# The second copy of the short lists' places: in three PSUM banks, or in the product's SBUF buffer

## The chip, the cores and the metric

One core of one Trainium2 chip runs the kernel once. The metric is the device time in microseconds (us); the runs of a kernel are compared by their median. The profile shows one execution: "span" is the time from the first to the last instruction of the program, less than the device time of a run.

Engines are named as in the profile: PE is TensorE, PEld its weight loads, DVE VectorE, ACT ScalarE, POOL GpSimd, SP SyncE. SBUF and PSUM are the two on-chip memories. PSUM is used here in banks of 512 float32 per partition, eight in all.

## The reference, cut to what matters

Two layers over 16 graphs of 1024 nodes with 64 channels. Layer 0 multiplies the adjacency (rows divided by their sums) with the normalised nodes. Layer 1 takes, for each node and channel, three quantiles over the node's neighbours, after some neighbours are dropped, and puts the weighted sum through a small network.

```python
# layer 0
h = jnp.maximum(_layernorm(x, axis=-1), 0.0)
x = x + jnp.matmul(A / clip(sum(A, 2), 1.0), h)
# layer 1
h = jnp.maximum(_layernorm(x, axis=-1), 0.0)
adj_d = _dilate_adj(adj, mask)            # drops every skip-th neighbour of long lists
vals = jnp.where((adj_d > 0)[..., None], h[:, None, :, :], big)
sv = jnp.sort(vals, axis=2)
for tau, wt in zip([0.25, 0.5, 0.75], [0.25, 0.5, 0.25]):
    q = gather(lo) * (1.0 - frac) + gather(hi) * frac   # lo, hi: places around tau * (m - 1)
    agg = agg + wt * q
x = x + relu((h + agg) @ W1 + b1) @ W2 + b2
```

`x` is (16, 1024, 64), `adj` (16, 1024, 1024), all float32; most nodes have few neighbours, a few have many.

## The kernel before, in words

The list path does the work; a dense path behind a flag runs only if a list overflows.

**Layer 0**, batch by batch: adjacency rows are loaded (`at`), ACT takes their signs (`sg`), DVE turns the signs into keyed neighbour lists (`rec`), PE transposes the rows into `pt` banks, ACT copies these to `att`, PE multiplies them with the nodes into a `ps_small` bank, and so on to a record per node (`row`). POOL scatters the records to DRAM (`srt`), sorted by list length, one indirect DMA for each 128 rows.

**Layer 1**, in four groups of four batches. A group's nodes are cut into ten classes by list length (the lists of `CAPS`); each class is a `Job` with T tiles of 128 nodes and n places each, the node itself included. There are 40 such short jobs. Four more jobs (`LONG`) take the longest lists of all batches. A job does this:

- POOL gathers each place's channels by an indirect DMA into `places` (`lplaces` for the long lists), one DMA for each place and tile, 124 in each group.
- DVE finds the dropped places (`rem`, `gone`, `ok`), ACT adds a huge number to them.
- DVE sorts along the places with a network of `tensor_tensor` min and max passes. A pass reads two runs of places and writes a third; so that a pass never overwrites what another still needs, each place exists in two copies: copy 0 is `places`, copy 1 is `other` (`long_other` for the long lists), copy 2 the node itself (`S`).
- DVE and ACT multiply the sorted places with the weights `w`, which gives `prod`. PE sums and transposes `prod` through an identity into a `pt` bank, and the small network follows in `ps_small` banks; POOL scatters the result (`out_dram`).

For the short lists `other` is one PSUM tile of three banks (`ps_o`), one buffer. For the long lists `long_other` lies in SBUF, and after about 0.8 us of passes (`BREATH`) a one-element memset of `idle` stands between them. `prod` (SBUF, two buffers) is taken after the passes, before the product. `pt` has two banks, `ps_small` three.

**The order** is made by a planner (`Plan`). Every stream of work yields an engine and the earliest time at which it could go on; the planner keeps a modelled clock for each engine and always issues the stream that could begin first. `room(name, bufs)` is that time for a buffer: infinite while its last users haven't released it. On DVE and POOL this order is kept as written; the instructions of ACT, PE and SP are ordered by the compiler's scheduler, by their data dependencies. All of these engines execute in order. All operations go through a recording helper, so that the profile has line 228 for nearly all of them, and groups are told apart by tile names.

The steps of the prediction can be followed at these places: the pools at the start of `list_path`; `transposes`, `products` and `layers`, which take `pt` and `ps_small`; `Job.sort`, which takes `other` and `prod`, makes the passes and the product; `Job.run`, which issues the gathers.

Of the kernel before, what the change touches and what calls it, by code (L numbers as in the profile page):

```python
# [9 lines left out]
F32 = mybir.dt.float32  # L10
# [8 lines left out]
P = 128  # L19
# [18 lines left out]
)  # L38
CAPS2 = [CAPS[1]] + CAPS[2::2]
LONG = (88, 31, 24, 20)  # L40
LSEG = 8
LCAPS = (24, 16, 16, 16)
LSUB = 8
# [168 lines left out]
INF = float("inf")  # L212
BREATH = 0.8
# [20 lines left out]
class Plan:  # L234
# [33 lines left out]
    def at(self, *tiles):  # L268
        return max(self.ready.get(t.tensor.name, INF) for t in tiles)
# [104 lines left out]
def list_path(ctx, tc, x, adj, nodemask, w1, b1, w2, b2, out, go):  # L374
# [23 lines left out]
    gat = ctx.enter_context(tc.tile_pool(name="gat", bufs=3))  # L398
    tiny = ctx.enter_context(tc.tile_pool(name="tiny", bufs=2))
    mlp = ctx.enter_context(tc.tile_pool(name="mlp", bufs=2))  # L400
    ps_t = ctx.enter_context(tc.tile_pool(name="ps_t", bufs=2, space=bass.MemoryType.PSUM))
    ps_s = ctx.enter_context(tc.tile_pool(name="ps_s", bufs=3, space=bass.MemoryType.PSUM))
    ps_o = ctx.enter_context(tc.tile_pool(name="ps_o", bufs=1, space=bass.MemoryType.PSUM))


    diff = consts.tile([P, P], I32, name="diff")
# [149 lines left out]
    def known(st, *names):  # L556

        return max(at(st[name]) if name in st else INF for name in names)
# [19 lines left out]
    def beginnings(pool, now):  # L578

        for b, st in enumerate(batch):  # L580
            now[0] = b
            yield "DVE", lambda: max(known(st, "xt", "mrow"), room("h0", 3), room("row", 4))
            mrow_f = new(tiny, [NT, P], F32, "mrow_f", 2)
            nc.vector.tensor_copy(mrow_f, st["mrow"])

            h0 = new(pool, [P, NT, C + 1], F32, "h0", 3, users=2)
            nc.vector.memset(h0[:, :, C:], 1.0)
            row = st["row"] = new(pool, [P, NT, RW], F32, "row", 4, users=1)
            nc.vector.memset(row[:, :, C:W], -1.0)
            yield from normed(h0[:, :, :C], st["xt"])  # L590
            st["h0"] = h0
            yield "PE", lambda: max(at(mrow_f), room("ps_small", 3))
            pm = new(ps_s, [P, HALF], F32, "ps_small", 3, users=1)
            nc.tensor.transpose(pm[:, :NT], mrow_f, ident[:NT, :NT])
            yield "ACT", lambda: at(pm)
            nc.scalar.copy(row[:, :, RW - 1], pm[:, :NT])
            nc.scalar.copy(row[:, :, RW - 2], row_f)
            free(pm)
# [58 lines left out]
    def transposes(pool, now):  # L657
        for b, st in enumerate(batch):
            now[0] = b
            for t in range(NT):  # L660
                hf, k = divmod(t, BPH)
                for h2 in range(2):
                    yield "PE", lambda: max(
                        at(st["rows"][t]) if t in st["rows"] else INF, room("pt", 2),
                        0.0 if hf in st["att"] else room("att", 2),
                    )
                    if hf not in st["att"]:
                        st["att"][hf] = new(pool, [P, NT, HALF], F32, "att", 2, users=1)
                    pt = new(ps_t, [P, HALF], F32, "pt", 2, users=1)
                    for q in range(BPH):  # L670
                        c0 = (h2 * BPH + q) * P
                        nc.tensor.transpose(
                            pt[:, q * P:(q + 1) * P], st["rows"][t][:, c0:c0 + P], ident
                        )
                    plan.add(turned(st, hf, k, h2, pt), 10 * b + 3)
                free(st["rows"][t])

    def products(pool, now):


        for b, st in enumerate(batch):
            now[0] = b
            for hf in range(2):
                yield "PE", lambda: INF if st["copied"][hf] < 2 * BPH else max(
                    at(st["att"][hf]), known(st, "h0"), room("ps_small", 3)
                )
                po = new(ps_s, [P, HALF], F32, "ps_small", 3, users=1)
                for q in range(NT):
                    if q and q % 2 == 0:
                        yield "PE", always  # L690
                    nc.tensor.matmul(
                        po[:C + 1, :], st["h0"][:, q, :], st["att"][hf][:, q, :],
                        start=(q == 0), stop=(q == NT - 1),
                    )
                free(st["att"][hf])
                free(st["h0"])
                yield "ACT", lambda: max(at(po), room("msg", 2))
                msg = new(pool, [C + 1, HALF], F32, "msg", 2)
                nc.scalar.copy(msg, po[:C + 1, :])
                free(po)  # L700
                yield "PE", lambda: max(at(msg), room("ps_small", 3))
                pb = new(ps_s, [P, HALF], F32, "ps_small", 3, users=1)
                sums = pb[:, :BPH * (C + 1)].rearrange("p (k c) -> p k c", c=C + 1)
                for k in range(BPH):
                    nc.tensor.transpose(
                        sums[:, k, :], msg[:, k * P:(k + 1) * P], ident[:C + 1, :C + 1]
                    )
                yield "DVE", lambda: at(pb) + SLACK
                x1 = st["row"][:, hf * BPH:(hf + 1) * BPH, X1:R0]
                deg = new(tiny, [P, BPH], F32, "deg", 2)  # L710
                nc.vector.tensor_scalar(deg, sums[:, :, C], 1.0, None, op0=OP.max)
                nc.vector.reciprocal(deg, deg)
                nc.vector.tensor_tensor(
                    x1, sums[:, :, :C], deg.unsqueeze(2).to_broadcast([P, BPH, C]), OP.mult
                )
                nc.vector.tensor_tensor(
                    x1, x1, st["xt"][:, hf * BPH:(hf + 1) * BPH, :], OP.add
                )
                free(pb)
                st["residual"] += 1  # L720
            free(st["xt"])
# [15 lines left out]
    def endings(pool, now):  # L737

        first = lambda rank: rank - 3000
        for b, st in enumerate(batch):  # L740
# [28 lines left out]
            nc.vector.tensor_tensor(  # L769
                hot, cls, d.unsqueeze(1).to_broadcast([P, CLS, NT]), OP.is_equal  # L770
            )
            yield "PE", lambda: max(at(hot), room("ps_small", 3))
            pc = new(ps_s, [P, HALF], F32, "ps_small", 3, users=1)
            K = CLS * NT
            flat = hot.rearrange("p c t -> p (c t)")
            nc.tensor.matmul(pc[:, :K], earlier, flat, start=True, stop=True)
# [54 lines left out]
    class Job:  # L831
# [50 lines left out]
        def sort(self):  # L882
# [41 lines left out]
            else:  # L924
# [10 lines left out]
            nc.scalar.activation(u, u, AF.Abs)  # L935
            nc.scalar.activation(u, u, AF.Relu, bias=wt0, scale=-QUANTILES[0][1])
            yield "DVE", lambda: max(
                at(A) + SLACK if helped else 0.0, room("prod", 2) if short else 0.0,
                room("other" if short else "long_other", 1),
            ), self.later  # L940
            if short:
                Bt = new(ps_o, [P, 3 * HALF], F32, "other", 1, users=1)
                other = Bt[:, :n * T * C].rearrange("p (k t c) -> p k t c", k=n, t=T)
            else:
                other = Bt = new(pool, [P, n, T, C], F32, "long_other", 1, users=1)

            def places(copy, run, shift=0):
# [16 lines left out]
            for op, ai, aj, dist, copy, run in ops:  # L964
# [9 lines left out]
                nc.vector.tensor_tensor(dst, a, c, op)  # L974
                plan.own = None
                done.update(((copy, i + shift), plan.clock["DVE"] + 0.15) for i in each)
                if not short:

                    since += 0.07 + len(each) * T * C * 1.04e-3
                    if since > BREATH:  # L980
                        nc.vector.memset(idle, 0.0)
                        since = 0.0
            yield "DVE", lambda: at(u) + SLACK, self.later

            w = new(pool, [P, count, T], F32, name + "w", bufs)
# [1 line left out]
            nc.vector.scalar_tensor_tensor(w, u[:, 2, :, :], 2.0, w, op0=OP.mult, op1=OP.add)  # L987
            free(u)

            total = max(count + 1, 4)  # L990
            prod = None
            if short:
                prod = new(pool, [P, T, total, C], F32, "prod", 2, users=1)
                if count + 1 < total:
                    nc.vector.memset(prod[:, :, count + 1:, :], 0.0)

            helped = plan.clock["ACT"] < plan.clock["DVE"] + 2.0
            for copy in (1, 0):
# [20 lines left out]
                    )  # L1019
            if short:  # L1020
                free(A)
                free(Bt)
                if not helped:
                    yield "ACT", lambda: at(S)
                nc.scalar.copy(prod[:, :, count, :], S[:, :, :C])
# [13 lines left out]
        def layers(self, terms, sources):  # L1039

            T, R = self.T, terms[0][0].shape[1]
            yield "PE", lambda: max(at(*sources) + LOOSE, room("y", 6), room("pt", 2))
            y = new(mlp, [P, T, CO], F32, "y", 6, users=1)
            x1 = y
            if self.short:
# [3 lines left out]
            for t0 in range(0, T, 4):  # L1049
                ts = range(t0, min(t0 + 4, T))  # L1050
                M = len(ts) * P
                if t0:
                    yield "PE", lambda: room("pt", 2)
                pt = new(ps_t, [P, HALF], F32, "pt", 2, users=1)
                for i, t in enumerate(ts):
                    for k, term in enumerate(terms[t]):
                        nc.tensor.matmul(
# [7 lines left out]
                ot = new(mlp, [2 * C, HALF], F32, "ot", 2)  # L1065
                nc.scalar.copy(ot[:R, :M], pt[:R, :M])
                free(pt)
                yield "PE", lambda: max(at(ot) + SLACK, room("ps_small", 3))
                ph = new(ps_s, [P, HALF], F32, "ps_small", 3, users=1)
                nc.tensor.matmul(ph[:, :M], w1_sb[:R, :], ot[:R, :M], start=True, stop=True)  # L1070
                yield "ACT", lambda: max(at(ph) + SLACK, room("hid", 2))
                hid = new(mlp, [H, HALF], F32, "hid", 2)
                nc.scalar.activation(hid[:, :M], ph[:, :M], AF.Relu, bias=b1_sb)
                free(ph)
                yield "PE", lambda: max(at(hid) + SLACK, room("ps_small", 3))
                py = new(ps_s, [P, HALF], F32, "ps_small", 3, users=1)
                pv = py[:, :len(ts) * CO].rearrange("p (t c) -> p t c", c=CO)
                nc.tensor.matmul(
                    py[:, :len(ts) * CO], ones_f[:1, :], b2_sb[:, :len(ts) * CO],
# [554 lines left out]
```

## Time and profile before

| | |
|---|---|
| runs | 1948.59, 1953.29, 1955.87 us; median 1953.29 |
| profiled execution, span | 1511.0 us; its own device time isn't recorded apart; the median lies 442.3 us above the span |
| PE, PEld busy | 738.8, 464.7 us |
| DVE busy | 1191.3 us (79%), 4104 instructions |
| ACT busy | 816.4 us (54%) |
| POOL busy | 957.2 us (63%), 1154 instructions, 931 of them indirect DMAs |
| DMA | 133.36 MB, 88 GB/s in the mean |
| granted PE clock, mean | 0.699 |

How to read it: layer 0 runs from the start to about 890 us, in the later part mixed with the jobs of the first groups; after that there are only jobs. The page's groups give operation, tiles, count, busy time, the mean of one in ns, and the engine's idle time in front of them with what ended it; "issue" is idle time in which the profile shows no wait. The busy tenths cut the span into 40 slices of 37.8 us.

### The profile page before, as it was taken

The page shows a single profiled execution, that of the slowest core. Times are in us where ns is not written, and L with a number is a line of the kernel's source. Part 1 is how long each engine was busy: PE and PEld are TensorE (multiplying, and loading weights), DVE is VectorE, ACT ScalarE, POOL GpSimd, SP SyncE. Part 2 cuts the span into 40 slices and gives each one's busy share as a digit, 9 for nine tenths or more (in the row PEclk, how much of TensorE's full clock was granted, in tenths as well). Part 3 has the DMA queues.
Part 4 walks back from the last instruction along what each step waited for, and adds up shares of the span by engine and source line. Part 5 has one row for each costly group of instructions (what it writes and reads, how often), then busy time and mean ns, then how long its engine had stood idle before and what let it go on. Part 6 is the DMA issues. An engine that isn't in the chain of part 4 may idle for free. (4 is left out here: it accounts for less than half of the span.)

```text
span 1511.0 us, 15983 instructions
## 1 busy us (share of the span) xinstructions
PE 738.8 (49%) x3192; PEld 464.7 (31%) x3192; DVE 1191.3 (79%) x4104; ACT 816.4 (54%) x2789; POOL 957.2 (63%) x1154
## 2 busy tenths in 40 slices
PE   4778777327877556567667620024000123228542
PEld 2434334214544233343444320012000122216432
DVE  6777798997899779859869869893059999986875
ACT  7989878557879457757975520201050223148341
POOL 0122227777678757757777787667777777765083
PEclk8889888658888777869688755555555565558765
DMA  5445665424355253355341242111111111211010
GB/s 177 150 142 168 163 210 160 123 73 114 101 162 152 59 174 94 99 126 161 94 140 31 60 101 68 50 37 28 30 26 23 28 28 40 44 33 22 2 25 13
DMA packets 135718, 133.36 MB, mean 88 GB/s; under 512 B 100756, under 2 KB 103444, under 8 KB 135492
## 3 DMA queue, kind: packets, MB, share of 16 engines
q1 hardware_dynamic: 102876, 90.79, 20.8%
q0 software_dynamic: 32736, 41.47, 11.2%
q14 instruction: 78, 0.64, 0.1%
q8 instruction: 28, 0.46, 0.1%
HBM read 112.90 MB, written 23.61 MB: 90 GB/s over the span
## 5 line engine op out<-in xcount | busy, mean ns | idle before, releaser
L228 POOL DMA_INDIRECT places<-tab,idx x372 | 370.2, 995 | 131.7 <-issue 101.8
L228 PE MATMUL pt<-ident,prod 128*128 128x128 f32 (+1 forms) x736 | 160.2, 377 | 517.8 <-DVE prod L228 241.2
L228 PEld LDWEIGHTS pt<-ident,prod 128*128 128x128 f32 (+1 forms) x736 | 129.3, 256 | 550.4 <-ACT prod L228 412.4
L228 PE MATMUL ps_small<-att,h 128*65 128x512 f32 x512 | 254.7, 644 | 27.3 <-ACT h L228 10.5
L228 POOL DMA_INDIRECT srt<-row,to x128 | 125.9, 984 | 165.8 <-ACT row L228 144.0
L228 PE MATMUL pt<-ident,at 128*128 128x128 f32 x1024 | 176.7, 320 | 96.0 <-ACT att L228 71.1
L228 POOL DMA_INDIRECT lplaces<-whole,lidx x163 | 167.2, 1026 | 55.6 <-issue 48.5
L228 DVE MAX8 rec<-sg 128x8 f16<-128x256 f16 x512 | 180.1, 414 | 4.4
L228 PEld LDWEIGHTS pt<-ident,at 128*128 128x128 f32 x1024 | 136.9, 164 | 143.5 <-ACT att L228 93.8
L228 ACT ACTIVATE sg<-at 128x1024 f16<-128x1024 f32 x128 | 134.8, 1054 | 75.0 <-DMA at<-in_adj_dram 65.7
L228 ACT COPY att<-pt 128x512 f32<-128x512 f32 x256 | 141.9, 582 | 20.7 <-PE pt L228 18.8
L228 POOL DMA_INDIRECT places<-tab,last_idx x124 | 123.8, 998 | 41.3 <-issue 35.0
L228 PEld LDWEIGHTS ps_small<-att,h 128*65 128x65 f32 x512 | 74.7, 151 | 161.9 <-issue 123.2
L228 ACT ACTIVATE places<-places,gone 128x64 f32<-128x64 f32 x496 | 123.5, 335 | 0.5
L228 ACT ACTIVATE prod<-places,w 128x64 f32<-128x64 f32 x213 | 54.1, 336 | 120.5 <-DVE w L228 120.5
L228 POOL DMA_INDIRECT out_dram<-y,nodes_i x93 | 91.8, 987 | 22.6 <-issue 15.1
L228 DVE TENSOR_TENSOR sg<-sg,keyed 128x1024 f16<-128x1024 f16 x128 | 87.2, 681 | 23.7 <-ACT sg L228 23.7
L228 ACT ACTIVATE gone<-gone 128x15 f32<-128x15 f32 (+9 forms) x40 | 8.2, 206 | 169.2 <-DVE ok L228 169.0
L228 DVE TENSOR_TENSOR long_other<-lplaces 128x512 f32<-128x512 f32 (+5 forms) x124 | 64.1, 555 | 29.1 <-ACT lplaces L228 28.9
L228 DVE TENSOR_TENSOR other<-places,other 128x64 f32<-128x64 f32 (+6 forms) x204 | 69.6, 341 | 5.9
L228 PE MATMUL ps_small<-ot,w_sb 128*128 128x128 f32 (+3 forms) x112 | 47.6, 513 | 44.2 <-DVE y L228 31.2
L228 DVE TENSOR_TENSOR places<-places,other 128x64 f32<-128x64 f32 (+2 forms) x208 | 62.3, 309 | 4.9
(231 smaller groups left out, 1670.8 us busy)
## 6 DMA issues: line engine op xcount, KB each, us to landing
at<-in_adj_dram SPq DMA_DIRECT2D x128, 512.0 KB
places<-tab,idx POOLq DMA_INDIRECT x372, 2.5
whole<-tab SPq DMA_DIRECT2D x4, 1057.0 KB
tab<-row SPq DMA_DIRECT2D x16, 264.0 KB
xt<-in_x_dram SPq DMA_DIRECT2D x16, 256.0 KB
lplaces<-whole,lidx POOLq DMA_INDIRECT x163, 2.4
srt<-row,to POOLq DMA_INDIRECT x128, 2.7
places<-tab,last_idx POOLq DMA_INDIRECT x124, 2.4
```

What stands on the lines that cost most here:

```text
L228: ins = getattr(self._engine, op)(*args, **kwargs)
```

## The change

The second copy of the short lists moves from PSUM to SBUF. `other` is now a view of the job's `prod` buffer, which is therefore taken before the passes and held through them; `ps_o` and its three banks go. The buffer is as large as the larger of the two uses. The product of copy 1 is made in place. The one-element memsets now stand between the passes of short lists too. Two of the three banks go to `pt` (2 to 4) and one to `ps_small` (3 to 4), and every `room` of these names follows. The gathers, the passes and their order within a job, the products and the long lists are as before.

```diff
+PT, SMALL = 4, 4
...
-    ps_t = ctx.enter_context(tc.tile_pool(name="ps_t", bufs=2, space=bass.MemoryType.PSUM))
-    ps_s = ctx.enter_context(tc.tile_pool(name="ps_s", bufs=3, space=bass.MemoryType.PSUM))
-    ps_o = ctx.enter_context(tc.tile_pool(name="ps_o", bufs=1, space=bass.MemoryType.PSUM))
+    ps_t = ctx.enter_context(tc.tile_pool(name="ps_t", bufs=PT, space=bass.MemoryType.PSUM))
+    ps_s = ctx.enter_context(tc.tile_pool(name="ps_s", bufs=SMALL, space=bass.MemoryType.PSUM))
...
-                        at(st["rows"][t]) if t in st["rows"] else INF, room("pt", 2),
+                        at(st["rows"][t]) if t in st["rows"] else INF, room("pt", PT),
...
-                    at(st["att"][hf]), known(st, "h0"), room("ps_small", 3)
+                    at(st["att"][hf]), known(st, "h0"), room("ps_small", SMALL)
...
             yield "DVE", lambda: max(
-                at(A) + SLACK if helped else 0.0, room("prod", 2) if short else 0.0,
-                room("other" if short else "long_other", 1),
+                at(A) + SLACK if helped else 0.0, room("prod", 2) if short else room("long_other", 1),
             ), self.later
+            total = max(count + 1, 4)
             if short:
-                Bt = new(ps_o, [P, 3 * HALF], F32, "other", 1, users=1)
-                other = Bt[:, :n * T * C].rearrange("p (k t c) -> p k t c", k=n, t=T)
+                prod = new(pool, [P, T, max(n, total), C], F32, "prod", 2, users=1)
+                other = prod.rearrange("p t k c -> p k t c")
             else:
+                prod = None
                 other = Bt = new(pool, [P, n, T, C], F32, "long_other", 1, users=1)
...
-                if not short:
-
-                    since += 0.07 + len(each) * T * C * 1.04e-3
-                    if since > BREATH:
-                        nc.vector.memset(idle, 0.0)
-                        since = 0.0
+                since += 0.07 + len(each) * T * C * 1.04e-3
+                if since > BREATH:
+                    nc.vector.memset(idle, 0.0)
+                    since = 0.0
...
-            total = max(count + 1, 4)
-            prod = None
-            if short:
-                prod = new(pool, [P, T, total, C], F32, "prod", 2, users=1)
-                if count + 1 < total:
-                    nc.vector.memset(prod[:, :, count + 1:, :], 0.0)
+            if short and count + 1 < total:
+                nc.vector.memset(prod[:, :, count + 1:total, :], 0.0)
...
             if short:
                 free(A)
-                free(Bt)
...
-                yield "PE", lambda: max(at(ot) + SLACK, room("ps_small", 3))
-                ph = new(ps_s, [P, HALF], F32, "ps_small", 3, users=1)
+                yield "PE", lambda: max(at(ot) + SLACK, room("ps_small", SMALL))
+                ph = new(ps_s, [P, HALF], F32, "ps_small", SMALL, users=1)
```

More of the change, by code (lines that the diff above doesn't have):

```diff
@@ L591, in beginnings @@
             st["h0"] = h0
-            yield "PE", lambda: max(at(mrow_f), room("ps_small", 3))
-            pm = new(ps_s, [P, HALF], F32, "ps_small", 3, users=1)
+            yield "PE", lambda: max(at(mrow_f), room("ps_small", SMALL))
+            pm = new(ps_s, [P, HALF], F32, "ps_small", SMALL, users=1)
             nc.tensor.transpose(pm[:, :NT], mrow_f, ident[:NT, :NT])
@@ L668, in transposes @@
                         st["att"][hf] = new(pool, [P, NT, HALF], F32, "att", 2, users=1)
-                    pt = new(ps_t, [P, HALF], F32, "pt", 2, users=1)
+                    pt = new(ps_t, [P, HALF], F32, "pt", PT, users=1)
                     for q in range(BPH):
@@ L684, in products @@
                 yield "PE", lambda: INF if st["copied"][hf] < 2 * BPH else max(
-                    at(st["att"][hf]), known(st, "h0"), room("ps_small", 3)
+                    at(st["att"][hf]), known(st, "h0"), room("ps_small", SMALL)
                 )
-                po = new(ps_s, [P, HALF], F32, "ps_small", 3, users=1)
+                po = new(ps_s, [P, HALF], F32, "ps_small", SMALL, users=1)
                 for q in range(NT):
@@ L700, in products @@
                 free(po)
-                yield "PE", lambda: max(at(msg), room("ps_small", 3))
-                pb = new(ps_s, [P, HALF], F32, "ps_small", 3, users=1)
+                yield "PE", lambda: max(at(msg), room("ps_small", SMALL))
+                pb = new(ps_s, [P, HALF], F32, "ps_small", SMALL, users=1)
                 sums = pb[:, :BPH * (C + 1)].rearrange("p (k c) -> p k c", c=C + 1)
@@ L771, in endings @@
             )
-            yield "PE", lambda: max(at(hot), room("ps_small", 3))
-            pc = new(ps_s, [P, HALF], F32, "ps_small", 3, users=1)
+            yield "PE", lambda: max(at(hot), room("ps_small", SMALL))
+            pc = new(ps_s, [P, HALF], F32, "ps_small", SMALL, users=1)
             K = CLS * NT
@@ L1041, in layers @@
             T, R = self.T, terms[0][0].shape[1]
-            yield "PE", lambda: max(at(*sources) + LOOSE, room("y", 6), room("pt", 2))
+            yield "PE", lambda: max(at(*sources) + LOOSE, room("y", 6), room("pt", PT))
             y = new(mlp, [P, T, CO], F32, "y", 6, users=1)
@@ L1052, in layers @@
                 if t0:
-                    yield "PE", lambda: room("pt", 2)
-                pt = new(ps_t, [P, HALF], F32, "pt", 2, users=1)
+                    yield "PE", lambda: room("pt", PT)
+                pt = new(ps_t, [P, HALF], F32, "pt", PT, users=1)
                 for i, t in enumerate(ts):
@@ L1074, in layers @@
                 free(ph)
-                yield "PE", lambda: max(at(hid) + SLACK, room("ps_small", 3))
-                py = new(ps_s, [P, HALF], F32, "ps_small", 3, users=1)
+                yield "PE", lambda: max(at(hid) + SLACK, room("ps_small", SMALL))
+                py = new(ps_s, [P, HALF], F32, "ps_small", SMALL, users=1)
                 pv = py[:, :len(ts) * CO].rearrange("p (t c) -> p t c", c=CO)
```

## The prediction

> **What bounds the kernel now.** I read the page's busy times and slices first, then POOL's and ACT's waits, then the timeline and group tables of single stretches.
>
> ```profile
> span 1511.0 us, 15983 instructions
> ...
> POOL 0122227777678757757777787667777777765083
> ...
> L228 POOL DMA_INDIRECT places<-tab,idx x372 | 370.2, 995 | 131.7 <-issue 101.8
> L228 POOL DMA_INDIRECT lplaces<-whole,lidx x163 | 167.2, 1026 | 55.6 <-issue 48.5
> ...
> L228 DVE TENSOR_TENSOR other<-places,other 128x64 f32<-128x64 f32 (+6 forms) x204 | 69.6, 341 | 5.9
> ```
>
> DVE has the highest busy share (79%), but look at POOL's slices: from the sixth on they stand at 7 to 8 tenths and don't move, whatever the others do. That is a full queue: a gather takes 0.95 us and 0.30 us of "issue" follow, and 0.95/1.25 is 76%. The timeline shows POOL's real waits (over 2 us): 213 us until the fourth batch is through layer 0, then, up to 1391 us, waits that sum to some 55 us, the longest 12.3, 9.2 and 7.0 us. So nearly all of 1178 us goes to some 850 indirect DMAs in a row. Behind it comes a tail of some 110 us, in which DVE sorts the last long lists.
>
> ```profile
> POOL srt L228 <- ACT row L228: 134.7, 8, 63.7
> ...
> ACT msg L228 <- PE ps_small L228: 4.7, 4, 1.9
> ...
> ACT att L228 <- PE pt L228: 3.4, 12, 0.4
> ```
>
> These are waits of the first 215 us. POOL's start is set by ACT (`row`), which is busy 86 and 89% in the first two hundreds of us; ACT waits for PE little.
>
> **The change part by part.** *Gathers beside the passes.* Today a short pass mostly has one operand in PSUM; after the change both are in SBUF, as in the long sort today. The trace shows what POOL makes of either. The first row is from 1230 to 1250 us, where DVE does nothing but a short sort (17.9 of 19.7 us busy), the second from 1119 to 1171 us, all long sort (51.9 of 52 us):
>
> ```profile
> L228 POOL DMA_INDIRECT places<-tab,last_idx x15 | 14.2, 945 | 4.6 <-issue 4.0 <-DMA places<-tab,last_idx 0.3 <-ACT places L228 0.3
> ```
>
> ```profile
> L228 POOL DMA_INDIRECT lplaces<-whole,lidx x35 | 41.8, 1195 | 10.7 <-issue 10.7
> ```
>
> A gather costs 250 ns more beside passes that read SBUF twice. In the timeline it is seen in each one:
>
> ```profile
> 508.75 0.48 DVE L228 TENSOR_TENSOR places<-places,other 128x128 f32<-128x128 f32 x2
> 508.92 0.94 POOL L228 DMA_INDIRECT places<-tab,idx  x1 [0.30 <-issue]
> ...
> 1142.95 0.68 DVE L228 TENSOR_TENSOR long_other<-lplaces 128x512 f32<-128x512 f32 x1
> 1142.97 0.06 DVE L228 MEMSET idle<- 128x1 f32 x1
> 1143.06 1.38 POOL L228 DMA_INDIRECT lplaces<-whole,lidx  x1 [0.30 <-issue]
> ```
>
> The memsets don't prevent it: they are in that stretch. Price from above: 35 gathers by 0.250 us in 52 us of passes is 0.168 us for each us of them. The passes that read `other` take 69.6 + 62.3 + 55.0 + 50.1 = 237 us (728 of them), the products from it 25.9 us: 263 us by 0.168 is 44 us. Price from below: short jobs already have passes with both inputs in SBUF (the first layers, 208 passes). Going through the timeline gather by gather, the 33 covered to more than 80% by such passes take 1034 ns in the mean, the 155 covered by passes that read PSUM 952 ns: 82 ns. Gathers lie beside PSUM-reading passes for 192.5 us in all, 202 gathers' worth: 17 us. The passes that change are 326 ns long in the mean (237/728), those 208 some 351 ns, the groups of the long ones 448 to 567 ns; so the lower row is the nearer, and I take 20 us. Not all reaches the end: the 55 us of waits behind 213 us can swallow a late POOL where the awaited work isn't late itself. I let a quarter vanish: **+15 us**, bounds +5 and +44.
>
> [...]
>
> *The passes themselves and the memsets.*
>
> ```profile
> L228 DVE TENSOR_TENSOR other<-places,other 128x64 f32<-128x64 f32 x88 | 20.1, 228 | 2.7
> ...
> L228 DVE TENSOR_TENSOR lplaces<-long_other 128x64 f32<-128x64 f32 x13 | 2.8, 218 | 0.0
> ...
> L228 DVE MEMSET idle<- 128x1 f32 x195 | 11.5, 59 | 0.0
> ```
>
> At equal width a pass gains 0 to 10 ns: 728 by 0.005 us is 4 us less DVE work. The rule of `BREATH`, applied to the ten pass lists of a group (234 passes), gives 60 memsets, 240 in all: 240 by 59 ns is 14 us more. Net +10 us on DVE, hidden where POOL is the later one; DVE is 85 to 91% busy from 200 to 600 us and so partly uncovered. I take **+5 us**, bounds 0 and +14.
>
> [...]
>
> *`prod` before the passes.* A sort now begins only when the `prod` of the job but one before has been read by PE. In the timeline, the first pass of a job comes 4.0 to 187 us after that point in all 38 cases, so the wait never binds in today's order: 0; without this cover at most one sort's length (299 us over 40 jobs: 7 us) for a job. Behind such a wait stands all of DVE, the listing of layer 0 among it.
>
> *ACT's copy of the node into `prod`.* It needs no sort today: it ran 0.4 to 167 us ahead of the job's weights in 38 of 40 jobs. In the seven classes with more places than products its slot is now a place being sorted, so ACT waits for passes there: a new wait, with copies to `att`, signs and the next job's masks queued behind it. The scheduler can put it late; ACT already waits for `w` in 13 jobs. I take 0; from above, 28 jobs by the 4.4 us that such a wait costs between 215 and 890 us (17.4 us, 4 times) is 123 us of ACT, which has some 200 us idle there: a quarter on the path is +30 us.
>
> *Two second copies, more banks.* With one `other` the next sort must follow the product before; a dozen jobs follow within 4 us, so there is nearly nothing to gain: -1 us. `pt` banks: over the whole span PE waits 74.4 us for ACT's `att` copies, but ACT only 18.8 us for PE; banks let PE run ahead of an engine that is already the later one. In the first 215 us the two ACT waits shown sum to 8 us, the most that POOL's start can gain. The fourth `ps_small` bank meets 42.7 us of PE waits for `y`, 7 times, 28.6 of them after 890 us, where PE has much idle time. I take **-4 us** for banks and copies, bounds 0 and -63 (8 plus all 55 us of POOL's waits).
>
> Sum: +15 + 5 + 0 + 0 - 4 = +16 us. The span goes from 1511.0 to 1527, and with the same 442.3 us around it the time from 1953.29 to **1969 us**. A difference counts as one from 0.5%, 9.8 us, on; no change is 1943.5 to 1963.1.
>
> **The rivals.** *The banks win (faster).* The fourth small bank frees the products and networks of layer 0 from waiting for `y`, records reach POOL earlier, and POOL's waits close. For it: 55 us of waits are there, several behind ACT and DVE results of layer 0. Against it: ACT and DVE, not banks, are the late ones. It decides when it brings more than 30 us (20 to cover the two costs, 10 to be seen): half of the 55 us and all 8 us at the start are 35, so 1953 + 20 - 35 = 1938 us. Chance 0.21.
>
> *Swallowed (no change).* Narrow passes hold POOL up by the lower price, 17 us, half vanishes in its waits, the memsets hide, the banks bring 4: 1953 + 8 - 4 = 1957 us. Against it: the waits that would swallow it end on DVE and ACT work that gets later too. Chance 0.19.
>
> *ACT stalls (much slower).* The node copy blocks ACT in layer 0 and adds its +30: 1953 + 16 + 30 = 1999 us. For it: the copies run far ahead today. Against it: ACT is only 54% busy. Chance 0.12.
>
> *The forecast*, a fuller POOL queue, 1963 to 1990 us: 0.48. Slower is thus 0.60, the same 0.19, faster 0.21. All orders are made anew by the planner, so that single waits move. The range is 1938 to 2000 us: down to the faster case, up to the ACT case. The forecast's own range is 1963 to 1990.
>
> **What would show it.** Right: gathers beside short sorts at 1030 to 1200 ns instead of 945; POOL's busy time up by 17 to 44 us at the same 931 indirect DMAs; some 435 `idle` memsets; POOL's start at 205 to 213 us; the tail as long as now. Wrong: gathers unchanged beside short passes; or POOL's waits behind 213 us well under 55 us, or a start before 200 us (the banks won); ACT waiting tens of us at the copy from `S` (the ACT case). The planner's new order alone could move a long list's sort into the tail or out of it, which I can't price.

## The result and the profile after

| | median | ratio to the kernel before, 95% interval |
|---|---|---|
| before | 1954.58 us (4 runs) | |
| changed | 2013.02 us (2007.68 to 2019.38, 4 runs) | 1.0307 [1.0280, 1.0334] |

The change costs 3.1%, some 60 us, against a forecast of 16 and a range that ended at 2000. One run of the experiments below, of the changed kernel, took 1660.91 us at a lower granted clock (0.529, the others 0.672 to 0.680) and is left out there. From the page of the changed kernel: span, POOL's tenths, and the two groups that answer to those shown of before (busy time, mean ns, idle time in front).

```profile
span 2005.7 us, 16248 instructions
...
POOL 0232643735371745555716465667577204653051
...
L229 POOL DMA_INDIRECT places<-tab,idx x372 | 364.0, 979 | 253.1 <-issue 106.5
...
L229 DVE TENSOR_TENSOR prod<-places,prod 128x64 f32<-128x64 f32 (+6 forms) x204 | 67.0, 335 | 29.5 <-remote 16.4
```

Nearly everything is wrong with this against the forecast. The gathers' mean fell (995 to 979 ns) where it should have risen, POOL is idle for 253 us in front of them instead of 132, its tenths swing between 1 and 7 where they were to stand still, and the span is 2 us below this execution's own 2007.68 us, not 442. The largest waits of POOL between 215 and 1400 us after the `issue` ones:

```profile
POOL places L229 <- ACT prod L229: 70.1, 4, 37.8
POOL gat_rows L229 <- DVE nodes_i L229: 44.6, 2, 27.0
POOL out_dram L229 <- DVE y L229: 44.4, 5, 27.9
```

POOL waits here for ACT and DVE in turn. The added memsets are as priced, 435 of 59 ns:

```profile
L229 DVE MEMSET idle<- 128x1 f32 x435 | 25.7, 59 | 0.7 <-DVE lplaces L229 0.7
```

### The profile page after: what moved, and what is told of

It is laid out like the page before. It is cut to its first block, busy times and chain, and to the rows that moved or that the text cites. A ratio compares the mean times of both kernels' runs of the same rounds, so it can differ in the third digit from the quotient of the medians.

```text
span 2005.7 us, 16248 instructions
## 1 busy us (share of the span) xinstructions
PE 793.3 (40%) x3192; PEld 508.8 (25%) x3192; DVE 1156.6 (58%) x4343; ACT 831.6 (41%) x2810; POOL 947.7 (47%) x1158
## 4 chain that ended last, share of the span: by engine, by line
DVE 29%; issue 21%; another core or an unknown queue 16%; ACT 13%; PE 11%; POOL 5%; DMA 3%; SPq 1%; DVEq 0%; POOLq 0%; ACTq 0%
PE ps_small L229 6%; PE pt L229 5%; DVE prod L229 5%; DVE places L229 4%; DVE long_other L229 3%; DVE lplaces L229 3%; ACT sg L229 3%; DVE rec L229 2%; POOL places L229 2%; ACT lplaces L229 2%; DMA at<-in_adj_dram 2%; ACT places L229 2%; ACT ln_sq L229 2%; ACT att L229 1%
## 5 line engine op out<-in xcount | busy, mean ns | idle before, releaser
L229 POOL DMA_INDIRECT places<-tab,idx x372 | 364.0, 979 | 253.1 <-issue 106.5
L229 PE MATMUL pt<-ident,prod 128*128 128x128 f32 (+1 forms) x736 | 179.4, 411 | 637.9 <-DVE prod L229 351.6
L229 PEld LDWEIGHTS pt<-ident,prod 128*128 128x128 f32 (+1 forms) x736 | 145.2, 286 | 671.1 <-DVE prod L229 285.4
L229 PE MATMUL ps_small<-att,h 128*65 128x512 f32 x512 | 263.1, 663 | 25.8 <-ACT att L229 17.7
L229 POOL DMA_INDIRECT srt<-row,to x128 | 130.0, 1016 | 204.0 <-ACT row L229 156.0
L229 POOL DMA_INDIRECT lplaces<-whole,lidx x163 | 158.8, 974 | 91.6 <-issue 49.4
L229 PEld LDWEIGHTS pt<-ident,at 128*128 128x128 f32 x1024 | 150.6, 174 | 200.7 <-ACT att L229 99.0
L229 PE MATMUL ps_small<-ot,w_sb 128*128 128x128 f32 (+3 forms) x112 | 56.1, 594 | 159.9 <-ACT ot L229 129.8
L229 ACT ACTIVATE prod<-places,w 128x64 f32<-128x64 f32 x234 | 59.3, 334 | 110.1 <-DVE w L229 94.5
L229 ACT COPY ot<-pt 128x128 f32<-128x128 f32 (+3 forms) x56 | 22.1, 396 | 198.8 <-remote 92.7
L229 DVE TENSOR_TENSOR prod<-places,prod 128x64 f32<-128x64 f32 (+6 forms) x204 | 67.0, 335 | 29.5 <-remote 16.4
```

Source lines behind the costliest of these rows:

```text
L229: ins = getattr(self._engine, op)(*args, **kwargs)
```

## The experiments

Each ratio is to the kernel before on the same chip at the same time. "Told" and "not told" is about the planner: whether its clock counts the memsets, and so whether they change the order that it makes.

### First: the kernel before once more, and one part undone or done alone

The kernel before, unaltered. 

> The kernel before, unchanged, profiled once more. Its first profile has a span of 1511.0 us, 442 us under its runs, and no stall on DVE without a releaser; the profile of the changed kernel has a span of 2005.7 us, 2 us under its run, and 341 us of DVE stalls (over 0.4 us) whose releaser the profile doesn't know. Theory A (stalls of the instruction supply: both kernels have them, and the first profile of before missed them): span 1945 to 1960 us, 250 to 350 us of such stalls on DVE. Theory B (the stalls are new with the change, and the 442 us lie outside the program): span 1505 to 1515 us again, no such stalls. Time ratio to before 1.00 in both.

Measured: 1952.57 us, 0.9988 [0.9964, 1.0012]. From its page (span, the chain's shares by engine, POOL's tenths, the gathers):

```profile
span 1952.3 us, 15983 instructions
...
POOL 0132355462555446356653655576677024574061
...
DVE 33%; ACT 18%; issue 15%; another core or an unknown queue 15%; PE 10%; POOL 5%; DMA 3%; SPq 0%; DVEq 0%; ACTq 0%; POOLq 0%
...
L228 POOL DMA_INDIRECT places<-tab,idx x372 | 359.0, 965 | 224.2 <-issue 107.3
```

The same kernel, with busy times on DVE, ACT and POOL that agree to some 2%, is 441 us longer than in the profile from which the prediction was made. Those 441 us are idle time inside the span, and for much of it the profile names no releaser: "issue" and "another core or an unknown queue" have 30% of the chain. Summed over the trace, gaps of DVE above 0.4 us without a known releaser are 254 us; in the first profile they were 2.5. Part of that can be the trace: it holds 10,504 semaphore updates where the first profile holds 25,405, and a wait whose update is missing has no releaser either. POOL's waits above 2 us behind 215 us sum to 597 us (44 of them) against 113 (13) by the same count. What it looks like, from the timeline, ACT masking a long list's places, here

```profile
1406.02 0.35 ACT L228 ACTIVATE lplaces<-lplaces,lgone 128x64 f32<-128x64 f32 x1 [1.05 <-issue]
...
1407.42 0.59 ACT L228 ACTIVATE lplaces<-lplaces,lgone 128x64 f32<-128x64 f32 x2 [1.05 <-issue]
...
1410.21 0.35 ACT L228 ACTIVATE lplaces<-lplaces,lgone 128x64 f32<-128x64 f32 x1 [1.05 <-issue]
```

and in the first profile:

```profile
1097.78 3.45 ACT L228 ACTIVATE lplaces<-lplaces,lgone 128x64 f32<-128x64 f32 x14
```

Fourteen in 3.45 us there, one or two at a time with a pause of 1.05 us here. A missing record doesn't explain these pauses: POOL had issued the gathers of the masked places 121 to 127 us earlier. So the page shown before and the times shown before are of two different situations. POOL is the bound in the first and not in the second. Theory A has its numbers; that the supply of instructions is what stands isn't shown.

Only the old banks (changed kernel otherwise):

```diff
-PT, SMALL = 4, 4
+PT, SMALL = 2, 3
```

> The changed kernel with pt and ps_small at 2 and 3 banks as before; three banks stay empty. If the new banks (through the planner's new order) cost the 58 us: ratio 1.00 to 1.01. If the move to SBUF, with its memsets and the buffer held through the passes, costs it: ratio 1.025 to 1.035. If the banks helped and hid part of the loss: above 1.035.

Measured: 1961.49 us, 1.0029 [0.9992, 1.0067].

Changed kernel without the short lists' memsets:

```diff
-                since += 0.07 + len(each) * T * C * 1.04e-3
+                if not short:
+                    since += 0.07 + len(each) * T * C * 1.04e-3
...
```

> The changed kernel without the memsets between short passes (239 DVE instructions less). If DVE is short of instructions or time, and the memsets add to it: ratio 1.015 or lower. If POOL is held up by passes that read SBUF twice and the memsets let it in: slower than the changed kernel, 1.035 or more, with gathers beside short passes well over 1044 ns. If neither matters: 1.025 to 1.035.

Measured: 1959.27 us, 1.0023 [0.9992, 1.0054].

The kernel before with these memsets (planner told), second copy in PSUM as ever:

```diff
-                if not short:
-
-                    since += 0.07 + len(each) * T * C * 1.04e-3
...
+                since += 0.07 + len(each) * T * C * 1.04e-3
...
```

> The kernel before with the memsets between the short passes too, the second copy still in PSUM. If the memsets alone cost the time (instructions on DVE): ratio 1.015 to 1.035. If they are hidden: 0.995 to 1.005. The forecast's term for them was +5 us with bounds of 0 and +14, that is 1.000 to 1.007.

Measured: 1982.21 us, 1.0136 [1.0079, 1.0193]. Taking out either the banks or the memsets removes the loss: parts that add up don't do that. What all three edits share is that they make the planner write a new order.

### Second: memsets in a fixed order, the move alone, ACT's wait

From here on the memsets can be issued past the planner (`tc.nc` instead of the recording `nc`), so that DVE's order stays as it is without them:

```diff
-                    nc.vector.memset(idle, 0.0)
+                    (tc.nc if short else nc).vector.memset(idle, 0.0)
```

In the changed kernel: 

> The changed kernel with the same rule for the short memsets, but the planner isn't told of them: DVE's order is that of the changed kernel without short memsets (1.002 of the kernel before), with some 240 memsets between its passes. A, the memsets themselves cost (instructions and stalls): 1.02 to 1.03, about 2000 us. B, the planner's other order costs, which its 0.04 us for each memset brings about: 1.000 to 1.008, the 240 memsets by 59 ns being at most 14 us (0.7%).

Measured: 1985.64 us, 1.0143 [1.0074, 1.0211].

In the kernel before: 

> The kernel before with some 240 memsets between its short passes, of which the planner isn't told, so that DVE's order is that of the kernel before (with the planner told it was 1.0136). A, memsets themselves: 1.01 to 1.02. B, order: 0.998 to 1.007.

Measured: 1982.25 us, 1.0150 [1.0099, 1.0201]. Both expectations had something: 240 memsets in an unchanged order cost 28 us in the kernel before, 0.12 us each, twice their 59 ns, and 23 us in the changed one (1.0143 against 1.0023). The rest of the changed kernel's loss, 1.0143 to 1.0307 or 32 us, comes with telling the planner.

The move to SBUF alone (old banks, no short memsets): 

> Only the move of the second copy into the product's SBUF buffer: two and three banks as before, no short memsets. The forecast's gather term would make it 1.005 to 1.01 by itself. A, passes that read SBUF twice and the new ACT wait cost next to nothing: 0.997 to 1.004, as with either more banks or memsets beside it. B, they do cost and more banks or memsets each gave it back: 1.01 to 1.02.

Measured: 1968.20 us, 1.0067 [1.0036, 1.0098], between the two.

The changed kernel with the node in slot 0 of `prod`, where no place is sorted:

```diff
-                prod = new(pool, [P, T, max(n, total), C], F32, "prod", 2, users=1)
-                other = prod.rearrange("p t k c -> p k t c")
+                prod = new(pool, [P, T, max(n + 1, total), C], F32, "prod", 2, users=1)
+                other = prod[:, :, 1:, :].rearrange("p t k c -> p k t c")
...
-                nc.scalar.copy(prod[:, :, count, :], S[:, :, :C])
+                nc.scalar.copy(prod[:, :, 0, :], S[:, :, :C])
```

> The changed kernel (1.031 of the kernel before) with the node's slot at the front of the product's buffer, in which no place is sorted; DVE's order is the same, and ACT's copy of the node waits for no pass. The 98 us that ACT stood before these copies go. A, that wait is a large part of the loss: 1.00 to 1.015. B, it only moves ACT's idle time: 1.025 to 1.035.

Measured: 2021.78 us, 1.0344 [1.0287, 1.0400]. ACT's idle time in front of these copies falls from 98.5 to 1.8 us, and nothing came back. ACT's wait exists but isn't this loss.

### Third and fourth: other chips, where the kernel before takes 1518 us

The next eight runs came to two other chips. There the kernel before takes 1518.46 and 1517.67 us, the time that belongs to the first profile. So the two situations don't belong to the kernel. They go with the chip, or with the time at which it was used: each chip had one batch of runs, which can't tell the two apart.

The kernel before without its 195 memsets between long passes, in its own order:

```diff
-                        nc.vector.memset(idle, 0.0)
+                        plan.note("DVE", "memset", (idle, 0.0), {})
```

> The kernel before without its 195 memsets between the passes of the long lists, in the same order on DVE (the planner is told of them as if they were there). 240 memsets added in an unchanged order made the kernel before 29 us slower, 0.12 us for each, twice their 59 ns. A, any instruction added to DVE costs this in these stretches, and the memsets bring nothing: 195 by 0.12 is 23 us, so 0.986 to 0.992. B, between long passes a memset lets POOL's gathers through and pays for itself: 0.998 to 1.01.

Measured: 1514.98 us, 0.9972 [0.9958, 0.9986], beside B and far from A. They cost 0.02 us each here.

The changed kernel, short memsets told to the planner but not issued (the same line as above, for short lists): 

> The changed kernel without its short memsets, of which the planner is told as if they were there: DVE's order is that of the changed kernel (1.031). Not told and not there it was 1.002, there but not told 1.014. A, order and memsets are separate costs that add up: 1.031 less 0.012 to 0.015 is 1.016 to 1.019. B, the two only cost together: 1.002 to 1.006.

Measured: 1556.36 us, 1.0254 [1.0234, 1.0274]. The expectation had been made for the other chips; what it says here follows below, beside the changed kernel itself.

The kernel before, `SLACK` 2.1 instead of 2.0: 

> The kernel before with one constant of the planner, SLACK, at 2.1 instead of 2.0 us: the same instructions in another order. A, the planner's order alone moves the time by a per cent or more, so that any change that touches its clocks has such a part: 1.006 to 1.03, or faster than 0.994. B, it doesn't: 0.995 to 1.005.

Measured: 1523.71 us, 1.0038 [1.0017, 1.0058]: B. This reordering costs 0.4%.

The second copy in SBUF, old banks, memsets not told: 

> Second copy in SBUF, two and three banks, with the short memsets but the planner not told of them: the order of the kernel that was 1.007 without them and, with them and the planner told, 1.003. A, memsets cost 1.2 to 1.5% in any order held fixed: 1.018 to 1.023. B, with the old banks memsets cost nothing: 1.002 to 1.010.

Measured: 1548.26 us, 1.0199 [1.0178, 1.0220], the number of A, but not for its reason, as the runs without memsets below show.

The changed kernel itself: 

> The changed kernel itself, unaltered. On a chip on which the kernel before takes 1954 us: 1.028 to 1.034 as before. On one on which it takes 1518 us, A, the forecast's terms hold there (POOL's gathers some 20 us longer in sum, DVE some 5 us) and waits of the new order come on top, as in the kernel with memsets and old banks (1.020) and the one with banks and without memsets (1.025): 1.018 to 1.035. B, the loss belongs to the stalls of the other chips: 1.000 to 1.010.

Measured: 1550.48 us (three runs), 1.0219 [1.0186, 1.0252]: A. From its page:

```profile
span 1550.8 us, 16248 instructions
...
POOL 0222257777577667775876877767877777772071
...
DVE 32%; POOL 17%; ACT 16%; PE 12%; issue 12%; DMA 9%; SPq 1%; DVEq 0%; POOLq 0%; ACTq 0%
...
L229 POOL DMA_INDIRECT places<-tab,idx x372 | 377.5, 1015 | 137.1 <-issue 106.2
```

No unknown queue in the chain, POOL at 7 tenths nearly throughout, gathers 20 ns longer than in the first profile: this is the picture from which the forecast was made.

The move alone: 

> Only the second copy in the product's SBUF buffer; no short memsets, two and three banks (1.007 where the kernel before takes 1954 us). Where it takes 1518 us, A, passes that read SBUF twice hold up POOL's gathers and POOL bounds: gathers at 1020 to 1050 ns in the mean instead of 1000 to 1004, POOL's busy time up by 20 to 40 us, ratio 1.012 to 1.025. B, they don't: gathers at most 1010 ns, ratio 0.997 to 1.006.

Measured: 1558.47 us, 1.0271 [1.0239, 1.0304], just above A's range, while the gathers' mean stays below it:

```profile
span 1558.5 us, 15992 instructions
...
L229 POOL DMA_INDIRECT places<-tab,idx x372 | 375.6, 1010 | 119.0 <-issue 106.4
...
L229 POOL DMA_INDIRECT places<-tab,last_idx x124 | 131.8, 1063 | 37.8 <-issue 36.3
```

The gathers of the last group, those with the least other work beside them, stand at 1063 ns instead of 998.

Without short memsets, new banks: 

> The changed kernel without short memsets, the planner not told of any (1.002 where the kernel before takes 1954 us). Where it takes 1518 us, A, the SBUF passes cost by POOL, and banks bring nothing: 1.012 to 1.026. B, the loss of the told but not issued memsets (1.025) was the order's: 0.998 to 1.008.

Measured: 1560.38 us, 1.0289 [1.0262, 1.0315], above A's range.

The kernel before with memsets not told: 

> The kernel before with 240 memsets between its short passes in its own order (1.015 where the kernel before takes 1954 us, twice what 59 ns each make). Where it takes 1518 us, A, a memset costs its 59 ns at most, partly hidden, and the other half belonged to the stalls: 0.998 to 1.007 (14 us is 0.9%). B, it costs twice as much there too: 1.012 to 1.02.

Measured: 1516.47 us, 0.9991 [0.9975, 1.0008]: A. A memset costs nothing here.

```profile
span 1512.5 us, 16224 instructions
...
L228 POOL DMA_INDIRECT places<-tab,idx x372 | 370.8, 997 | 129.8 <-issue 103.0
```

Taken together, on these chips every kernel with the second copy in SBUF loses 2.0 to 2.9%. Banks bring nothing (1.0271 and 1.0289). The memsets, which cost nothing in the PSUM kernel, give part back: 1.0271 to 1.0199 in one order; in another 1.0254 to 1.0219, which is within the intervals. The gathers show why. Taking the gathers of short lists beside which sort passes and products sum to 80% of their length or more, instruction by instruction (where passes overlap, both count; counting the overlap once moves no mean by more than 8 ns):

| kernel | covered gathers, mean ns | gathers without a pass beside them |
|---|---|---|
| before | 967 (146) | 1016 |
| move alone | 1067 (114) | 992 |
| move and memsets, old banks | 1015 (118) | 994 |
| changed, memsets told but not issued | 1118 (117) | 1003 |
| changed | 1045 (113) | 1007 |

Beside passes that read SBUF twice a gather does take longer, by 78 ns in the changed kernel and by 100 with the move alone. With memsets between the passes, in the same order, it takes less again: 1015 instead of 1067 ns, and 1045 instead of 1118.

### Fifth: the move in the order of the kernel before

The planner's choices of the kernel before were written out as a list and replayed, so that DVE and POOL have that kernel's order:

```diff
-            entry = min(self.streams, key=begin)
+            pick = next(ORDER)
+            entry = next(e for e in self.streams if e[3] == pick)
...
-            helped = plan.clock["ACT"] < plan.clock["DVE"] + 2.0
+            helped = next(HELPED)
```

> The second copy in the product's SBUF buffer, two and three banks, no short memsets, and on DVE and POOL the order of the kernel before, choice by choice. Where the kernel before takes 1518 us, A, SBUF passes hold up POOL's gathers, and that is the loss: gathers at 1020 ns or more in the mean, 1.012 to 1.028. B, the planner's new order is the loss: 0.997 to 1.006, whatever the gathers take. C, half and half: gathers longer, 1.007 to 1.012. Where it takes 1954 us: 0.995 to 1.005 by all of them.

Measured, on a chip where the kernel before takes 1953.35 us: 1919.79 us, 0.9829 [0.9803, 0.9854]. No expectation had a gain. The gathers are longer here too (987 ns against the 965 above), and yet it is faster:

```profile
span 1907.9 us, 15975 instructions
...
L229 POOL DMA_INDIRECT places<-tab,idx x372 | 367.1, 987 | 168.2 <-issue 107.3
```

What ACT waits for before it writes `prod`:

```profile
ACT prod L229 <- DVE places L229: 33.8, 4, 17.8
ACT prod L229 <- DVE prod L229: 29.1, 3, 18.0
```

The same with the node first: 

> The same, with the node's slot at the front of the product's buffer, so that ACT's copy of the node waits for no pass. If ACT's wait has a part in the loss, this is faster than the run without it by 0.5% or more; if not, the two are within 0.3% of each other.

Measured: 1909.87 us, 0.9768 [0.9741, 0.9795]. These two waits are gone from the list, and the time is 0.5% below the run without it, about the size set beforehand. This version beats both kernels on such a chip, by 43 us the one before. On a chip where that takes 1518 us neither of the two was run.

The order's share is shown by the pair 0.9829 and 1.0067, from two such chips: the same banks and tiles, the same instructions but for 13 products that ACT makes more and 4 small memsets on POOL, and 46 us apart. What the planner does with the second buffer can be read from the order it writes. In the kernel before, the 936 short passes come in 40 blocks, one for each job. With the move, 10 of the 40 jobs have passes of another job between their own (14 in the changed kernel), and 349 instead of 327 gathers stand before the fourth group's first step. That the interleaving itself is the harmful part of the order wasn't tried.

## Why the prediction was wrong

**The premise.** The step that failed first is "with the same 442.3 us around it". There is nothing around the span: it lies within some 2 us of its execution's time in the profiled runs of both kernels. The 442.3 us were the difference between the two situations. That alone would have been harmless if the rest scaled, but POOL as the bound belongs to the 1518 us chips, and the two kernels were compared where POOL waits some 600 us. Even on the 1518 us chips the change costs 33 us (2.2%), twice the forecast of 16. POOL's tenths were also read too evenly: from the seventh slice, not the sixth, they lie between 5 and 8.

**The gather term** (+15, priced at 20 before a quarter was let go). The mechanism was right and the size nearly so, on the chips that it was read from: POOL's busy time went from 957.2 to 974.1 us, +17, and the lower price of 82 ns for a covered gather met 78.

```profile
PE 759.3 (49%) x3192; PEld 496.1 (32%) x3192; DVE 1150.4 (74%) x4343; ACT 818.9 (53%) x2810; POOL 974.1 (63%) x1158
```

Where the two kernels were compared it doesn't decide: POOL's busy time there is 947.7 us in the changed kernel and 935.9 in the one before.

**The passes** (-4 us). Wrong by a factor of ten, for a reason worth more than the rest. I compared the mean durations of single passes, and these hardly differ. The timeline shows it; first the kernel before, then the move alone, the same passes of the same width (start and duration in us):

```profile
506.19 0.29 DVE L228 TENSOR_TENSOR places<-places,other 128x128 f32<-128x128 f32 x1
506.52 0.29 DVE L228 TENSOR_TENSOR other<-places,other 128x128 f32<-128x128 f32 x1
506.85 0.29 DVE L228 TENSOR_TENSOR places<-places,other 128x128 f32<-128x128 f32 x1
507.17 0.30 DVE L228 TENSOR_TENSOR other<-places,other 128x128 f32<-128x128 f32 x1
```

```profile
523.55 0.28 DVE L229 TENSOR_TENSOR places<-places,prod 128x128 f32<-128x128 f32 x1
523.75 0.28 DVE L229 TENSOR_TENSOR prod<-places,prod 128x128 f32<-128x128 f32 x1
523.96 0.28 DVE L229 TENSOR_TENSOR places<-places,prod 128x128 f32<-128x128 f32 x1
524.16 0.28 DVE L229 TENSOR_TENSOR prod<-places,prod 128x128 f32<-128x128 f32 x1
```

0.29 against 0.28 us each, but a step from start to start of 0.33 against 0.20. In the kernel before a pass with PSUM in it mostly begins 34 ns after the end of the one before; with the move alone mostly some 80 ns ahead of that end. Over the pairs of neighbouring short passes that both touch the second copy the mean goes from +18 (694 pairs) to -56 ns (677), 74 ns less; by 728 passes that is an estimate of 54 us. DVE's busy time, in which overlapping instructions count once, falls by 40 us, from 1191.3 to the 1151.2 of this line from the page of the move alone:

```profile
PE 762.4 (49%) x3192; PEld 482.7 (31%) x3192; DVE 1151.2 (74%) x4104; ACT 820.4 (53%) x2802; POOL 981.1 (63%) x1158
```

The run in the old order fits this: DVE is busy 39 us less (1194.6 to 1155.5) and 34 us of the time are gained. That the one is the cause of the other is the likeliest reading, not tried apart; the move alone in its new order has the same 1155.5 us and no gain. On the 1518 us chips no run shows the gain.

**Memsets** (+5, bounds 0 and +14). Count and duration were right; the price depends on the chip: -1 us of 240 in one order where the kernel before takes 1518 us, 23 to 28 us where it takes 1954.

**`prod` before the passes and two second copies** (0 and -1 us). This is the mis-sized term that decides. I priced the wait for a buffer and the chance of an earlier start, but not that a second buffer lets the planner mix two sorts. The order that follows costs 46 us where the two kernels were compared. The prediction's last sentence named the planner's order as what it couldn't price; it could have been bounded by the order itself.

**ACT's copy of the node** (0, upper +30). ACT stands 98.5 us before these copies in the changed kernel. It costs 10 us in the old order and nothing that can be told in the new one.

**Banks** (-4). From 1.0067 to 1.0023, -9 us, on the one kind of chip, from 1558.47 to 1560.38 us on the other, both within the intervals. With the memsets told to the planner the same banks go with a loss of 54 us (1.0029 to 1.0307). The rival in which the banks win is out.

In us of 1954, the chain of runs is: move in the old order -33, the planner's order for it +46, banks -9, memsets +23, the planner told of them +32; sum +59, and 60 were measured. The sum has to come out, since each step begins where the one before ends; another path gives the parts other sizes, as the 54 us of the banks show. The intervals leave each step uncertain by 5 to 15 us, and the steps come from several chips, each against its own runs of the kernel before.

**What stays open.** Whether the move in the old order also gains, or loses, on a 1518 us chip; its loss of 2.0 to 2.9% there has the longer gathers (+16 to +33 us of POOL's busy time) and the new order in it (POOL's waits above 2 us sum to 132 to 153 us instead of 113), not separated. Why the new order costs what it does where the two kernels were compared. And what makes the same kernel lose 436 us on some chips.

## What to carry to other kernels

Before working from a profile, hold its span against the times that the change will be judged by: a gap of 442 us meant that page and times came from two different situations, and the bound was another one in each. Price back-to-back instructions by the step from start to start, here 0.33 against 0.20 us, not by their mean duration, here 0.29 against 0.28. Where a planner or scheduler writes the order, a change that gives it a buffer is also a new order: replay the old one to see what the change itself does, which here turned the move alone from a loss of 0.7% into a gain of 1.7%.

## What the hardware did that was not expected

The same kernel took 1953 to 1955 us on three chips and in the comparison of the two kernels, and 1518 us on two. Granted clocks don't explain it alone (0.642 and about 0.695 in the mean; ACT's masks above went from a quarter of a us each to 1.4). On the slower chip of the timeline above ACT's masks stand although the gathers of what they read were issued 121 to 127 us before, and most of the loss comes after the first 200 us: the records of the first four batches are scattered by 78, 111, 149 and 185 us against 78, 110, 145 and 178, those of the sixteenth by 1152 against 889. The trace there also holds fewer records, 10,504 semaphore updates instead of 25,405 for the same kernel. A memset cost twice its length on one of the slower chips (0.12 us for 59 ns) and nothing on one of the others (240 of them, 1516.47 against 1517.67 us). What holds the engines up there isn't shown by any run.
